# Output rows stored in the order e mod 8, then e div 8, with a DRAM pattern of 16 x 8 rows

## Chip, cores, metric

One core of one Trainium2 chip. The metric is the device time of one execution in microseconds (us); lower is better.

## The reference

For each of the 496 pairs (i, j) of 32 fields, a 1024 x 128 slice of the input is multiplied by a 128 x 128 matrix, and the product is multiplied element by element with the other slice.

```python
# inputs (1024, 32, 128) f32, W (496, 128, 128) f32; I_IDX, J_IDX: the pairs i < j
v_i = inputs[:, I_IDX, :]
v_j = inputs[:, J_IDX, :]
transformed = jnp.einsum('bpd,ped->bpe', v_i, W)
return transformed * v_j            # (1024, 496, 128) f32
```

The output alone has 260 MB.

## The kernel before

An output tile holds e (128 rows of the output of a pair) on the partitions, and for two pairs (`OG = 2`) all 1024 batch elements: 8 KB per partition, 1 MiB per tile. Four such tiles rotate. SyncE issues the stores, the weight loads and nearly all loads of x. The host reorders the result to the reference's layout; this is not timed.

```python
opool = ctx.enter_context(tc.tile_pool(name="o", bufs=4))
...
def load_w(c, splits=(0, WL)):                     # 256 KB: WL = 4 matrices
    ...
        nc.sync.dma_start(out=w_raw[c][:, a:b, :], in_=wt[c, :, a:b, :])
...
def second(u):
    ...
    if k == 0 and h == 0:
        ots[g] = opool.tile([P, OG, BT], F32, tag="ot", name=f"ot_{g}")
    nc.vector.tensor_tensor(ots[g][:, k, s], po.pop(u), x_sb[j][:, s], ALU.mult)
    if q >= NQ - 2:                                # the last two pairs in smaller pieces
        nc.sync.dma_start(out=out[g, :, k, s], in_=ots[g][:, k, s])
    elif k == OG - 1 and h == 1:
        nc.sync.dma_start(out=out[g], in_=ots[g])
...
args.append(nc.dram_tensor("out_0_dram", (NQ // OG, P, OG, BT), F32, kind="ExternalOutput").ap())
...
y[:, perm, :] = got.transpose(3, 0, 2, 1).reshape(BT, NQ, P)
```

## Time and profile before

| | before |
|---|---|
| median | 766.67 us (765.97 to 773.16, 4 runs) |
| DMA engines busy | over 90% in all slices but the last |
| moved | 310 MB, 402 GB/s |
| store of 1 MiB, issue to landing | 8.9 us (median) |
| rows of 8 KB (packet records) | mean 320 ns, median 309; 92% at or under 330, 191 of 31616 at 600 to 609 |
| packets of 2 KB and more in flight (packet records, 20 to 750 us) | 16 in 75% of the time, 15 to 17 in 96% |

The prediction shows the lines that say what bounds the kernel. Three more are needed for the comparison later. The first is from the page's groups (busy us, mean ns; then the idle time just before these instructions and what ended most of it), the second from the page's DMA issues (KB each, us to landing), the third from the view of the output tile (duration of SyncE's issue of a store, ns min/median/max):

```profile
L172 DVE TENSOR_TENSOR ot<-po,x 128x512 f32<-128x512 f32 x992 | 618.6, 684 | 129.5 <-DMA out_dram<-ot 70.2
...
out_dram<-ot SPq DMA_DIRECT2D x247, 1024.0 KB, 8.9
```

```profile
L176 SPq DMA_DIRECT2D out_dram<-ot x247: 332/332/1258, 14.3 to 759.0; - x124
```

### The profile page before, as it was taken

To read this page: it belongs to the slowest core of one execution; us is meant where nothing else is said; L and a number is where in the kernel's file an instruction comes from. 1 tells how busy PE (TensorE), PEld (TensorE's weight loads), DVE (VectorE), ACT (ScalarE), POOL (GpSimd) and SP (SyncE) were. 2 spreads that over 40 slices of the span, in tenths; PEclk is the share of its full clock that TensorE was granted. 3 is DMA by queue.
4 is the path that set the end of the run, shared out by engine and by line. 5 is a ranking of instruction groups with operands and counts; after the bars stand their busy time and mean duration, and the time that the engine had idled before them with its cause. 6 is when DMAs were issued, how large, how long until landed. Compare 5 with 4: busy or idle time off the path is not lost.

```text
span 769.8 us, 11824 instructions
## 1 busy us (share of the span) xinstructions
PE 722.7 (94%) x2946; PEld 545.4 (71%) x2946; DVE 632.0 (82%) x1012; ACT 638.7 (83%) x1256; POOL 593.2 (77%) x863
## 2 busy tenths in 40 slices
PE   7988999999999999999999989999999999999994
PEld 3556766677777676777777767777777777777773
DVE  4869888888888788888888878888888888888885
ACT  2276988888888898888888889998988898998983
POOL 2677998887889878878878696978786969697660
PEclk9999999999999999999999999999999999999998
DMA  9999999999999999999999999999999999999997
GB/s 352 424 419 384 407 397 410 405 400 406 410 405 403 400 409 416 409 379 421 411 414 407 412 403 406 411 407 408 415 410 395 408 410 409 409 408 405 400 401 307
DMA packets 59108, 310.11 MB, mean 403 GB/s; under 512 B 6560, under 2 KB 6816, under 8 KB 27424
## 3 DMA queue, kind: packets, MB, share of 16 engines
q1 hardware_dynamic: 58464, 308.31, 99.4%
q10 hardware_dynamic: 576, 1.05, 0.4%
q8 instruction: 24, 0.39, 0.2%
q14 instruction: 44, 0.36, 0.1%
HBM read 49.28 MB, written 260.05 MB: 402 GB/s over the span
## 4 chain that ended last, share of the span: by engine, by line
DMA 61%; DVE 21%; PE 15%; issue 2%; DVEq 0%; SPq 0%; ACT 0%
DMA out_dram<-ot 60%; DVE ot L172 19%; PE po L157 9%; PE po L166 4%; DVE xd L195 2%; PE po L154 1%; DMA x<-in_xt_dram 1%; DVEq L172 0%; SPq L85 0%; DVEq L217 0%; ACT po L158 0%; DVEq L195 0%
## 5 line engine op out<-in xcount | busy, mean ns | idle before, releaser
L172 DVE TENSOR_TENSOR ot<-po,x 128x512 f32<-128x512 f32 x992 | 618.6, 684 | 129.5 <-DMA out_dram<-ot 70.2
L158 ACT ACTIVATE po<-po 128x512 f32<-128x512 f32 x962 | 551.2, 583 | 106.5 <-PE po L157 53.3
L157 PE MATMUL po<-xh,wh 128*128 128x512 f32 x962 | 388.7, 404 | 24.4 <-DVE ot L172 21.6
L166 PE MATMUL po<-xd,wd 128*128 128x512 f32 x962 | 376.9, 392 | 5.7 <-DVE xd L195 5.7
L157 PE MATMUL po<-xl,wl 128*128 128x512 f32 x962 | 377.6, 392 | 2.2 <-POOL wl L95 2.1
L157 PEld LDWEIGHTS po<-xh,wh 128*128 128x128 f32 x962 | 180.9, 188 | 110.2 <-DVE ot L172 72.5
L95 POOL TENSOR_TENSOR wl<-w,wh 128x256 fp32r<-128x256 f32 x241 | 179.2, 744 | 92.1 <-ACT wh L94 90.7
L166 PEld LDWEIGHTS po<-xd,wd 128*128 128x128 f32 x962 | 181.0, 188 | 46.3 <-ACT po L158 3.8
L157 PEld LDWEIGHTS po<-xl,wl 128*128 128x128 f32 x962 | 181.1, 188 | 36.8 <-POOL wl L95 4.5
L97 POOL TENSOR_TENSOR wd<-wl,wd 128x256 fp32r<-128x256 f32 x241 | 180.0, 747 | 20.1
L96 POOL TENSOR_SCALAR wd<-wh 128x256 fp32r<-128x256 f32 x241 | 99.1, 411 | 20.3
L94 ACT ACTIVATE wh<-w 128x256 fp32r<-128x256 f32 x241 | 99.2, 412 | 0.5 <-DMA w<-in_wt_dram 0.5
L110 POOL TENSOR_TENSOR xl<-x,xh 128x512 fp32r<-128x512 f32 x52 | 67.3, 1293 | 19.8 <-ACT xh L109 19.5
L115 POOL TENSOR_TENSOR xd<-xh,xl 128x512 fp32r<-128x512 f32 x32 | 41.4, 1292 | 2.7
L109 ACT ACTIVATE xh<-x 128x512 fp32r<-128x512 f32 x52 | 32.5, 628 | 10.5 <-DMA x<-in_xt_dram 10.3
L111 POOL TENSOR_SCALAR xl<-xl 128x512 fp32r<-128x512 f32 x52 | 32.8, 631 | 4.6
L154 PE MATMUL po<-x,w 128*128 128x512 f32 x60 | 29.0, 645 | 4.1 <-DMA x<-in_xt_dram 4.1
L154 PEld LDWEIGHTS po<-x,w 128*128 128x128 f32 x60 | 12.1, 206 | 20.2 <-issue 13.9
L195 DVE TENSOR_TENSOR xd<-xh,xl 128x512 fp32r<-128x512 f32 x20 | 16.6, 831 | 0.0
L109 ACT ACT_TABLE_LOAD x1 | 1.3, 1283 | 2.6 <-issue 2.6
L211 POOL MEMSET const-float32-0.0<- 128x1 f32 x1 | 0.1, 98 | 0.2 <-issue 0.2
L211 POOL MEMSET const-bfloat16-1.0<- 128x1 bf16 x1 | 0.1, 101 | 0.0
(2 smaller groups left out, 0.2 us busy)
## 6 DMA issues: line engine op xcount, KB each, us to landing
out_dram<-ot SPq DMA_DIRECT2D x247, 1024.0 KB, 8.9
w<-in_wt_dram SPq DMA_DIRECT2D x123, 256.0 KB, 9.1
x<-in_xt_dram SPq DMA_DIRECT2D x30, 512.0 KB, 9.5
x<-in_xt_dram ACTq DMA_DIRECT2D x4, 256.0 KB, 5.1
out_dram<-ot SPq DMA_DIRECT2D x4, 256.0 KB, 7.0
w<-in_wt_dram SPq DMA_DIRECT2D x1, 192.0 KB, 3.6
w<-in_wt_dram SPq DMA_DIRECT2D x1, 64.0 KB, 2.9
```

What stands on the lines that cost most here:

```text
L94: nc.scalar.mul(h, raw, 1.0 - 2.0**-13)
L95: nc.gpsimd.tensor_tensor(l, raw, h.bitcast(F32), ALU.subtract)
L96: nc.gpsimd.tensor_scalar(d, h.bitcast(F32), EPS, 1.0, ALU.mult, ALU.mult)
L97: nc.gpsimd.tensor_tensor(d, l.bitcast(F32), d.bitcast(F32), ALU.subtract)
L109: nc.scalar.mul(h, x_sb[f][:, s], 1.0 - 2.0**-13)
L110: nc.gpsimd.tensor_tensor(l, x_sb[f][:, s], h.bitcast(F32), ALU.subtract)
L115: nc.gpsimd.tensor_tensor(d, h.bitcast(F32), l.bitcast(F32), ALU.subtract)
L154: nc.tensor.matmul(po[u], w_raw[q // WL][:, q % WL, :], x_sb[i][:, s], start=True, stop=True)
L157: nc.tensor.matmul(po[u], w_s[c][t][:, r], x_s[i][t][:, s], start=t == 0, stop=t == 1)
L158: nc.scalar.mul(po[u], po[u], 1.0 + EPS)
L166: nc.tensor.matmul(po[u], w_s[q // WC][2][:, r], x_s[i][2][:, s], start=False, stop=True, skip_group_check=True)
L172: nc.vector.tensor_tensor(ots[g][:, k, s], po.pop(u), x_sb[j][:, s], ALU.mult)
```

## The change

Its intent is that adjacent rows of DRAM are written at any one time; no record shows which rows are. Row e of a tile goes to place (e mod 8) x 16 + e div 8.

```diff
-            nc.sync.dma_start(out=out[g, :, k, s], in_=ots[g][:, k, s])
+            nc.sync.dma_start(out=out[g, :, :, k, s].rearrange("b a c -> a b c"), in_=ots[g][:, k, s])
         elif k == OG - 1 and h == 1:
-            nc.sync.dma_start(out=out[g], in_=ots[g])
+            nc.sync.dma_start(out=out[g].rearrange("b a k c -> a b k c"), in_=ots[g])
...
-    args.append(nc.dram_tensor("out_0_dram", (NQ // OG, P, OG, BT), F32, kind="ExternalOutput").ap())
+    args.append(nc.dram_tensor("out_0_dram", (NQ // OG, 8, P // 8, OG, BT), F32, kind="ExternalOutput").ap())
...
-    y[:, perm, :] = got.transpose(3, 0, 2, 1).reshape(BT, NQ, P)
+    y[:, perm, :] = got.transpose(4, 0, 3, 2, 1).reshape(BT, NQ, P)
```

Two things change at once: where a row lands, and the shape of the store's DRAM side, from 128 rows to 16 x 8 rows. The shape is called the split below.

## The prediction

It rests on an assumption that the trace of before does not show: with a DRAM side of 16 x 8 rows, the 16 DMA engines fall into eight pairs whose rows hinder each other, so that a row takes twice 309 ns while a pair is in step. Its d is a second assumption: how far a pair is out of step, from 0 (a row takes 309 x 2 ns) to 1 (309 ns), by the form 309 x (2 - d). Three more are assumed: that all engines start a store together, which keeps d small (but in the trace of before the 16 landings of a store lie 4.7 us apart in the median); that with four buffers a pair which runs ahead loses its lead at the next store; and that a store therefore takes as long as its slowest pair. The long rows of which it speaks can be counted: of 1147 rows over 400 ns, 957 belong, in the order of starts, to the stores ahead of a weight load.

> **What bounds the kernel now.** I read the page from the top: the busy shares, the row of DMA shares, the queues, the chain that ended last, then the stretches and the waits. From the page of the kernel before:
>
> ```profile
> span 769.8 us, 11824 instructions
> PE 722.7 (94%) x2946; PEld 545.4 (71%) x2946; DVE 632.0 (82%) x1012; ACT 638.7 (83%) x1256; POOL 593.2 (77%) x863
> ...
> DMA  9999999999999999999999999999999999999997
> ...
> q1 hardware_dynamic: 58464, 308.31, 99.4%
> ...
> HBM read 49.28 MB, written 260.05 MB: 402 GB/s over the span
> ## 4 chain that ended last, share of the span: by engine, by line
> DMA 61%; DVE 21%; PE 15%; issue 2%; DVEq 0%; SPq 0%; ACT 0%
> DMA out_dram<-ot 60%; DVE ot L172 19%; PE po L157 9%; PE po L166 4%; DVE xd L195 2%; PE po L154 1%; DMA x<-in_xt_dram 1%; DVEq L172 0%; SPq L85 0%; DVEq L217 0%; ACT po L158 0%; DVEq L195 0%
> ```
>
> The reader is to see that the 16 DMA engines have no free slice, that one queue fills 99.4% of them, that five sixths of the bytes are stores, and that the store is 60% of the chain. TensorE at 94% looks as tight, but the chain gives it only 15%. Three lines of the table of stretches say that this holds all through (stretch, busy of PE, PEld, DVE, ACT, POOL, then clock, DMA share, GB/s):
>
> ```profile
> 100.00:200.00 100.00, 93.82 (x390) 71.49 (x389) 85.44 (x139) 85.39 (x172) 84.60 (x121) 1.00 1.01 404
> 300.00:400.00 100.00, 96.38 (x398) 72.78 (x397) 81.90 (x133) 87.83 (x173) 80.76 (x119) 1.00 1.01 407
> 600.00:700.00 100.00, 98.31 (x416) 76.85 (x416) 86.05 (x139) 90.09 (x177) 81.08 (x123) 1.00 1.01 408
> ```
>
> The chain in order of time shows the loop of the four output buffers (start us, us, what): a store of 1 MiB takes 8.9 us to land, four products of VectorE refill the buffer, and the next store starts.
>
> ```profile
> 601.03 8.94 DMA out_dram<-ot
> 610.10 2.50 DVE ot L172 x4
> 612.61 8.92 DMA out_dram<-ot
> 621.65 2.50 DVE ot L172 x4
> 624.16 8.93 DMA out_dram<-ot
> ```
>
> One round is 11.58 us and moves four stores and two weight loads, 4.72 MB, so 407 GB/s, as the stretches say. The 8.9 us are mostly queueing behind other stores. The page does not hold the packet records, so I counted them in the trace. A packet is one row. Each of the 247 large stores has 128 rows of 8 KB, so each of the 16 DMA engines moves 247 x 8 = 1976 of them:
> - 8 KB rows: median 309 ns[...]; mean 320; 92% at or under 330. Sum over 16 engines: 632.9 us.
> - 2 KB rows: mean 86 ns, 90.2 us. 4 KB rows: mean 173 ns, 41.4 us. Semaphore writes and instruction fetches: some 5 us.
>
> The sum, 770, is the span. So the time is the sum of the row times on each DMA engine, and anything that changes the time of an 8 KB row goes straight into it.
>
> [...]The trace of before shows 16 packets in flight nearly always[...]8192 B in 309 ns is 26.5 GB/s, and 92% of the rows run at it, so there are no lasting collisions.[...]
>
> **The change part by part.**
> *Removed and added instructions:* none. The order of the changed program against the old one has the same rows on TensorE, VectorE, ScalarE and GpSimd, and the same 405 on SyncE; only the stores differ, with a DRAM side of 16x8x2048 in place of 128x2048. Rows stay 8 KB long, so packets stay 31,616. The transposes in the host code are not timed.
>
> *Issuing:* SyncE may take longer over a pattern with one more dimension. It has room; this line of its waits (us in total, times, longest) is idle time:
>
> ```profile
> SPq L176 <- DVE ot L172: 481.8, 244, 4.4
> ```
>
> Even 0.5 us more for each of 251 stores is 126 us of 482. Cost 0.
>
> *Which engine moves which row:* here lies my choice. The outer DRAM dimension, e div 8, now has 16 values for 16 engines[...]
>
> *Cost in step:* a row takes twice 309, say 606 ns (a value at which rows of the kernel before already pile up when something halves them). 1976 x 606 = 1197 us; with 90 + 41 + 5 for the rest 1333 us.
>
> *Does it stay in step?* [...]So the slowest of eight pairs decides. I set d = 0.15, an estimate: 309 x 1.85 = 572 ns, 1976 x 572 = 1130 us, with 136 for the rest 1266. The timed runs lie 3.7 us under the profiled span (766.1 against 769.8): about 1262.
>
> *HBM side:* sixteen adjacent rows of 8 KB at once instead of rows far apart. The most that better placement could save is the excess over the floor: (320 - 309) x 1976 = 22 us, and I saw that the long rows sit in the last one or two of a store ahead of a weight load, which row order does not touch. I count 0.
>
> **The rivals.**
> - *[...]nothing happens.* [...]For it: rows, packets and bytes are the same, and 92% of the rows are at the floor, so HBM order can do nothing. [...]Time 760 to 772.
> - *The intent works: adjacent rows ease HBM.* All the excess saved is 22 us of 766, 2.9%; TensorE, 98% busy late on, would catch some. Time 745 to 760. Against it: where the long rows stand.
> - *Pairs drift out of step.* With d near a half a row takes 1.5 x 309 = 464 ns: 916 + 136 = 1052. In full opposition the loss is nil. [...]Against it: the slowest pair decides.
> - *HBM is worse too:* all engines in one stretch of 128 KB at the same offset in their rows. Then above 1340. Nothing in the profile speaks for it.
>
> **Range and chances.** The mechanism with d between 0 and 0.5 gives 1050 to 1333; I give it 0.72. Weaker conflicts, 800 to 1050: 0.12. No conflict: 0.13, a sliver of it faster. Worse than 2x: 0.03. Range 970 to 1345. Faster by over 2%: 0.02; within 2%: 0.12; slower: 0.86.
>
> **What would show it.** Right: packets and bytes as before, DMA share still 9 in every slice, but some 240 GB/s; 8 KB rows with a median near 570 to 606 ns; 2 KB and 4 KB rows unchanged; landing of a store about 18 us instead of 8.9; VectorE's wait for the store some 500 us instead of 70; TensorE's instructions as before with idle time between them. Wrong on the split: 8 KB rows still at 309. Wrong on d: rows split between 309 and 606 in equal numbers. Wrong on HBM: rows above 606, or loads slower too.

## The result, and the profile after

848.56 us median (845.13 to 851.18, 4 runs). The ratio to the kernel before is 1.1053, 95% interval 1.0995 to 1.1111. Ratios here are the mean time of one kernel's fast runs over that of the other's of the same rounds, so not quite the ratio of the medians. The change is slower by a tenth: the direction was predicted, the size was not.

From the page of the changed kernel, the lines that answer those of before:

```profile
span 845.2 us, 11824 instructions
PE 747.6 (88%) x2946; PEld 542.0 (64%) x2946; DVE 633.3 (75%) x1012; ACT 649.4 (77%) x1256; POOL 594.6 (70%) x863
...
DMA  9999999999999999999999999999999999999998
...
q1 hardware_dynamic: 58464, 308.31, 100.0%
...
HBM read 49.28 MB, written 260.05 MB: 366 GB/s over the span
...
DMA out_dram<-ot 70%; DVE ot L172 16%; PE po L157 6%; PE po L166 3%; DMA w<-in_wt_dram 1%; DMA x<-in_xt_dram 1%; DVE xd L195 1%; DVEq L172 0%; POOL xd L115 0%; POOL xl L110 0%; ACTq L76 0%; POOL wd L97 0%; POOL wl L95 0%; POOL xl L111 0%; DVEq L217 0%
...
L172 DVE TENSOR_TENSOR ot<-po,x 128x512 f32<-128x512 f32 x992 | 619.5, 684 | 203.8 <-DMA out_dram<-ot 134.3
...
out_dram<-ot SPq DMA_DIRECT2D x247, 1024.0 KB, 10.3
```

Packets (58464) and bytes are the same, the DMA engines are as full as before, yet they move 366 GB/s instead of 402. VectorE's products take the same 684 ns each and wait 134.3 us for stores instead of 70.2. So the same transfers keep the DMA engines busy for longer. The table of stretches shows it in every stage (same columns as in the prediction):

```profile
100.00:200.00 100.00, 88.94 (x363) 66.55 (x362) 79.90 (x129) 80.78 (x161) 75.44 (x108) 0.99 1.01 362
300.00:400.00 100.00, 90.74 (x364) 66.14 (x365) 76.15 (x123) 81.42 (x159) 75.35 (x109) 1.00 1.01 370
600.00:700.00 100.00, 93.11 (x372) 67.25 (x371) 76.74 (x125) 83.71 (x162) 72.70 (x107) 1.00 1.01 366
```

And the loop of the four buffers in the chain of the changed kernel, in order of time; a round takes 13.1 us here (594.19 to 607.32) instead of 11.6:

```profile
594.19 10.49 DMA out_dram<-ot
...
604.80 2.50 DVE ot L172 x4
...
607.32 10.95 DMA out_dram<-ot
```

The packet records of the two traces say which transfers got longer (one packet is one row; sums are over all packets, divided by 16 engines):

| rows | before: mean ns, sum us | after: mean ns, sum us |
|---|---|---|
| 8 KB (stores) | 320, 632.9 | 362, 716.1 |
| 2 KB (nearly all weight loads) | 86, 90.2 | 86, 90.1 |
| 4 KB (loads of x) | 173, 41.4 | 162, 38.9 |

All of the loss is in the stores' rows. Their median is still 309 ns; 8% were over 330 ns before, 18% are now, and 10% of all now lie between 500 and 850 ns.

The records do not name the DMA engine, but the trace holds 16 semaphore increments for each store. I take them as one from each of the 16 engines, when its share has landed. These are the 16 landings of the first three large stores, in us after the first landing of each (from the semaphore records):

```
before  store 1  0 .01 .05 .07 .23 .27 .36 .36 .41 .42 .43 .45 .48 .49 .65 1.26
        store 2  0 .01 .03 .06 .18 .24 .33 .34 .40 .41 .42 .44 .45 .46 .62 1.30
        store 3  0 .02 .03 .07 .18 .23 .32 .35 .38 .40 .40 .42 .45 .47 .61 1.41
after   store 1  0 .04 .10 .10 .11 .20 .26 .29 .32 .32 .34 .37 .40 .41 .44 .53
        store 2  0 .04 .06 .07 .08 .17 .26 .29 | 1.66 1.67 1.72 1.74 1.82 2.04 2.18 2.19
        store 3  0 .04 .08 .13 .15 .25 .27 .30 | 1.79 1.86 2.04 2.05 2.07 2.21 2.22 2.30
```

From the second store on, the landings of the changed kernel mostly come in two groups of eight. Over all 247 stores the gap between the eighth and the ninth landing has a median of 1.23 us (1 us or more in two thirds of the stores); before it is 0.05 us. Eight pairs in which one engine lags its partner would give this. A lag of just four rows (4 x 309 ns = 1.24 us) is not shown: the gap is the distance between the groups, and if the landings are matched in order (first with ninth, second with tenth and so on), the median lag is 1.84 us, six rows.

### The profile page after: what moved, and what is told of

It is laid out like the page before. It is cut to its first block, busy times and chain, and to the rows that moved or that the text cites. A ratio compares the mean times of both kernels' runs of the same rounds, so it can differ in the third digit from the quotient of the medians.

```text
span 845.2 us, 11824 instructions
## 1 busy us (share of the span) xinstructions
PE 747.6 (88%) x2946; PEld 542.0 (64%) x2946; DVE 633.3 (75%) x1012; ACT 649.4 (77%) x1256; POOL 594.6 (70%) x863
## 3 DMA queue, kind: packets, MB, share of 16 engines
q1 hardware_dynamic: 58464, 308.31, 100.0%
## 4 chain that ended last, share of the span: by engine, by line
DMA 72%; DVE 16%; PE 9%; issue 1%; POOL 1%; DVEq 0%; ACTq 0%; ACT 0%; SPq 0%; POOLq 0%
DMA out_dram<-ot 70%; DVE ot L172 16%; PE po L157 6%; PE po L166 3%; DMA w<-in_wt_dram 1%; DMA x<-in_xt_dram 1%; DVE xd L195 1%; DVEq L172 0%; POOL xd L115 0%; POOL xl L110 0%; ACTq L76 0%; POOL wd L97 0%; POOL wl L95 0%; POOL xl L111 0%; DVEq L217 0%
## 5 line engine op out<-in xcount | busy, mean ns | idle before, releaser
L172 DVE TENSOR_TENSOR ot<-po,x 128x512 f32<-128x512 f32 x992 | 619.5, 684 | 203.8 <-DMA out_dram<-ot 134.3
L158 ACT ACTIVATE po<-po 128x512 f32<-128x512 f32 x962 | 553.6, 582 | 170.9 <-PE po L157 107.1
L157 PE MATMUL po<-xh,wh 128*128 128x512 f32 x962 | 399.2, 415 | 72.6 <-DVE ot L172 67.3
## 6 DMA issues: line engine op xcount, KB each, us to landing
out_dram<-ot SPq DMA_DIRECT2D x247, 1024.0 KB, 10.3
w<-in_wt_dram SPq DMA_DIRECT2D x123, 256.0 KB, 10.3
```

What stands on the lines that cost most here:

```text
L157: nc.tensor.matmul(po[u], w_s[c][t][:, r], x_s[i][t][:, s], start=t == 0, stop=t == 1)
L158: nc.scalar.mul(po[u], po[u], 1.0 + EPS)
```

## The experiments

Theory P is that of the prediction: with a DRAM side of 16 x 8 rows the engines hinder each other in pairs over the partitions that they read, whatever the order of the rows in DRAM. Its first rival, H, is that sixteen adjacent rows written at once are slow in HBM. After both had been tested, the question was why the loss is 11% and not the 74% of engines that stay in step (1333 us in the prediction).

### 1. Split and order taken apart

`e1_split_only`: the new split, the old order, with one unused row after each eight. The issue of a store takes 551 ns (median) as in the changed kernel, not 332.

```diff
-            nc.sync.dma_start(out=out[g], in_=ots[g])
+            nc.sync.dma_start(out=out[g, :, 0:8], in_=ots[g])
...                     # the last two pairs and the host's reordering likewise
-  (NQ // OG, P, OG, BT)
+  (NQ // OG, 16, 9, OG, BT)
```

> The stores' DRAM side is 16 x 8 rows as in the changed kernel, but rows keep the old order (e div 8, then e mod 8, each block of 8 rows followed by one unused row[...]). Theory P[...]: 835 to 860 us as the changed kernel, landings of one store in two groups of eight about 1.2 us apart, 8 KB rows with a mean near 360 ns. Theory H (sixteen adjacent rows written at once are slow in HBM): 760 to 775 us, mean near 320 ns, though the landings may be in two groups.

`e2_order_only`: the changed kernel with e mod 4 and e div 4 in place of 8, so a DRAM side of 32 x 4.

```diff
-  (NQ // OG, 8, P // 8, OG, BT)
+  (NQ // OG, 4, P // 4, OG, BT)
```

> Rows in the order e mod 4, then e div 4, with a DRAM side of 32 x 4[...]. Theory P: 760 to 775 us, no two groups of eight among the landings, 8 KB rows near 320 ns. Theory H: 835 us or more, 8 KB rows near 360 ns. A gain by adjacency, the intent of the change: 745 to 760 us.

`e3_pattern_control`: as e1, but 32 x 4 rows (`out[g, :, 0:4]` of a tensor with 32 x 5 rows).

> Control: DRAM side of 32 x 4 rows in the old order, one unused row after each four. If the mere third dimension or the unused rows cost anything, it shows here. P and H both: 760 to 775 us, the 332 ns of the store's issue on SyncE may grow without effect.

`e4_loads_too`: the changed kernel, with the loads of x and w given a DRAM side of 16 x 8 as well. If the loss needs loads and stores of different splits, 770 to 800 us; if stores alone make it, 840 to 860 us.

```diff
-  in_=wt[c, :, a:b, :]
+  in_=wt[c, :, :, a:b, :].rearrange("b a q e -> a b q e")      # likewise for xt; the host lays both out to suit
```

> The changed kernel with the loads of x and w split in the same way as its stores (their DRAM rows stored e mod 8 first, DRAM side 16 x 8). [...]about 770 to 800 us. If it comes from the pairs of stores alone: 840 to 860 us, or more, as the loads now collide among themselves too (2 KB rows above 84 ns for one in five or so).

| run | us, median | ratio to before (95%) | 8 KB rows, mean ns | gap of landings 8 to 9, median us |
|---|---|---|---|---|
| the change | 848.56 | 1.1053 (1.0995 to 1.1111) | 362 | 1.23 |
| e1_split_only | 845.23 | 1.1026 (1.1003 to 1.1048) | 360 | 1.16 |
| e2_order_only | 768.61 | 1.0037 (1.0003 to 1.0071) | 317 | 0.03 |
| e3_pattern_control | 766.83 | 1.0007 (0.9982 to 1.0033) | 317 | 0.04 |
| e4_loads_too | 848.62 | 1.1075 (1.1030 to 1.1120) | 357 | 0.46 |

All four gave correct results. Span, and the row of the DMA issues for the stores, of e1 and then of e2:

```profile
span 844.3 us, 11824 instructions
...
out_dram<-ot SPq DMA_DIRECT2D x247, 1024.0 KB, 10.3
```

```profile
span 763.7 us, 11824 instructions
...
out_dram<-ot SPq DMA_DIRECT2D x247, 1024.0 KB, 8.9
```

The split alone makes the whole loss (1.1026), the order alone none of it (1.0037): H falls. The intent of the change gains nothing in e2 either. The issue of a store takes longer with the three-dimensional pattern (median 332 ns before, 545 ns in e2), without effect on the time. In e4 the loads' rows get longer too (4 KB rows with a mean of 199 ns instead of 162), the stores' rows are a little shorter (a mean of 357 ns), and the total stays: giving loads and stores the same split does not bring the time back.

### 2. Is it the partitions?

`m3_ports` moves data only: 60 stores of 64 partitions back to back, with the first partition at 0, 16, 32 and 0 again. The author took it that under P all rows hinder each other from partition 0 on, half of them from 16 and none from 32. Its output is wrong, which doesn't matter for the time.

```python
for base in (0, 16, 32, 0):
    for n in range(60):
        nc.sync.dma_start(out=out[g, 0:4].rearrange("b a k c -> a b k c"), in_=ots[n % 4][base : base + 64])
        g += 1
    gate()       # VectorE touches all four tiles: the next phase starts when all have landed
```

> Data movement alone, wrong result on purpose: four phases of 60 stores of 64 partitions (512 KB, 16 x 4 rows of 8 KB[...]), back to back; the partitions are 0-63, 16-79, 32-95, and 0-63 again. [...]rows near 606 ns and 2.4 us per store for 0-63, near 600 for half of the rows with 16-79, 309 ns and 1.25 us per store for 32-95. If something else of the new split is to blame (one more dimension, neighbouring rows): the same time in all four phases.

| partitions | us per 512 KB store | 8 KB rows: under 350 ns / over 550 ns |
|---|---|---|
| 0-63 | 2.57 | 5% / 94%, median 629 ns |
| 16-79 | 2.53 | 52% / 48% |
| 32-95 | 1.26 | 98% / 2%, median 309 ns |
| 0-63 again | 2.52 | 3% / 95%, median 628 ns |

The table of stretches of this run (columns: length, busy of DVE and POOL, clock, DMA share, GB/s), one stretch in each phase:

```profile
40.00:160.00 120.00, 0.34 (x2) 0.00 (x0) 1.00 0.99 206
200.00:300.00 100.00, 0.00 (x0) 0.00 (x0) 1.00 0.76 219
340.00:400.00 60.00, 0.69 (x4) 0.00 (x0) 1.00 1.01 384
430.00:520.00 90.00, 0.00 (x0) 0.00 (x0) 1.00 0.97 206
```

The same pattern and bytes run at 206 or at some 400 GB/s depending on the first partition alone. From partition 0 on a row takes some 629 ns, from 32 on 309, and from 16 on half of the rows (48%) are long. (In the stretch from 340 us on the end of the phase drags the mean; 512 KB in 1.26 us are 416 GB/s.) With 16-79 the DMA share is 0.76, so there some engines are idle part of the time; the trace does not say which. So collisions that follow the partitions as expected are shown; at what place on the chip the rows meet, and which engine takes which partition, is not, as no record names either.

### 3. In step, and out of step

`m_before` and `m_after`: data movement alone, with the stores in the old and in the changed form. The code is condensed. `gate()` is as above; because it goes through the tiles in order, three of four stores in the phases with a gate after each start alone, and the fourth starts behind its predecessor.

```python
for n in range(40): gate(); store(g, ots[n % 4]); g += 1          # 1: one at a time
gate()
for n in range(80): store(g, ots[n % 4]); g += 1                  # 2: back to back
gate()
for n in range(80):                                               # 3: a 256 KB load after every second
    store(g, ots[n % 4]); g += 1
    if n % 2 == 1: load_w(n // 2)
gate()
for n in range(20): store(g, ots[n % 4]); g += 1; load_w(40 + n); gate()     # 4
```

P1 is that stores hinder each other and that pairs which get out of step get free; P2 that stores do not hinder each other, but a load that is under way does.

> No arithmetic, wrong result on purpose: stores of 1 MiB in the old form in four phases. (1) 40 stores one at a time, each waited for; (2) 80 stores back to back; (3) 80 stores with a 256 KB weight load after every second; (4) 20 times one store and one load together, waited for. All theories: 8 KB rows at 309 ns in phases 1 and 2, 2.45 to 2.5 us per store in phase 2; the turn to a load in phases 3 and 4 stretches the last one or two rows.

> The same with the stores in the changed form. Theory P1[...]: phase 1 rows near 606 ns, as every store starts with all engines in step, and a store lands some 2.4 us later than in the old form; phase 2 starts slow and gets to 2.5 us per store when the pairs have drifted apart, landings in two groups of eight. Theory P2[...]: phases 1 and 2 as in the old form, 309 ns, and only phases 3 and 4 slower, with 8 KB rows of 500 to 800 ns while loads run.

| phase | us per store, old form | changed form | 8 KB rows, mean ns, old / changed |
|---|---|---|---|
| 1 one at a time | 3.89 | 5.88 | 318 / 473 |
| 2 back to back | 2.50 | 2.51 | 315 / 315 |
| 3 with loads | 2.86 | 3.27 | 313 / 365 |
| 4 store and load together | 4.42 | 6.40 | 372 / 522 |

From the chain in order of time, stores that start alone, m_before and then m_after (start us, us from issue to landing):

```profile
47.29 3.87 DMA out_dram<-ot
...
51.53 3.86 DMA out_dram<-ot
```

```profile
109.95 6.19 DMA out_dram<-ot
...
116.51 6.19 DMA out_dram<-ot
```

A stretch of phase 1, 2 and 3 each, m_before and then m_after:

```profile
40.00:170.00 130.00, 13.29 (x134) 0.00 (x0) 1.00 0.67 276
200.00:360.00 160.00, 0.00 (x0) 0.00 (x0) 1.00 1.01 419
400.00:590.00 190.00, 0.17 (x1) 0.00 (x0) 1.00 1.02 421
```

```profile
40.00:240.00 200.00, 13.33 (x136) 0.00 (x0) 1.00 0.65 178
280.00:440.00 160.00, 0.00 (x0) 0.00 (x0) 1.00 1.01 420
500.00:690.00 190.00, 0.00 (x0) 0.00 (x0) 1.00 1.01 367
```

A store that starts alone takes 2.3 us longer (6.19 against 3.86). By the packet records of the stores at 109.95 us (m_after) and 51.53 us (m_before), 0.4 us of this is a later first row (1.20 us after the issue instead of 0.83), and 2.0 us are longer rows, where a full doubling would be 2.47 us (8 x 309 ns). Most of the first rows take 596 to 640 ns. But the doubling does not last through even one store: in the order of their starts, the first 64 of its 128 rows have a mean of 629 ns, the last 64 of 401, and many of these are at 309 again. So the collision is partly over after 64 of the 128 rows, four per engine if each moves eight.

Back to back the changed form loses nothing: 420 GB/s against 419, rows with a mean of 315 ns in both. The landings of a store then spread over 2.8 us without a gap in the middle (eighth to ninth 0.26 us); matched in order, the lag is 1.28 us, about four rows. Pairs that no longer hinder each other at such a lag would give this. Two things keep it from being shown. The records name no engine. And in `m4_after` (section 5) the third to the sixth store, back to back, have all 16 landings within 0.8 to 0.9 us, so no pair can lag by four rows at the landing, and yet the rows between 17.5 and 27.5 us have a mean of 312 ns; there the lag grows to 1.22 us only in the course of 40 stores. How small a lag already avoids the collision, and why, stays open. So does the very first store of the changed kernel: its first 96 of 128 rows, in the order of their starts, took 309 to 318 ns, and its landings came within 0.53 us, where stores that start alone in the data-movement run took some 600 ns for their first rows. It was issued at 13.6 us and its first rows came at 19.7 us, behind loads; whether that is why was not tested.

With a load after every second store the loss is back at 0.41 us per store (3.27 - 2.86), and the rate of 367 GB/s is that of the full changed kernel. P1 holds, as far as it says that stores hinder each other and get free of it, though not in two groups of landings; P2 (loads alone collide with stores) falls with phase 1.

Around one load in phase 3 of m_after the packet records show how it goes. I counted the rows under way every 0.2 us. Between loads 16 rows are at 309 ns (563.0 to 564.4 us). In the 1.4 us before the first engines come to their load, eight rows are long and eight are not. While eight engines load (from 566.2 us), the eight other rows are long, and for some 1.2 us after it eight are long and eight are not. Then the other engines load, some seven rows are long once more for 0.6 us, and 16 are fast again. Whether each engine has its long rows once per load, the roles exchanged, can't be told without the engines' names.

### 4. What of a load costs?

`m2_before` and `m2_after`: six phases of 40 stores each.

```python
for every, many in ((1, 1), (2, 1), (4, 1), (4, 2)):       # phases 1 to 4: loads after so many stores, so many loads
    ...
# 5: as phase 2, with the load split as the changed stores: wt[c].rearrange("(b a) q e -> a b q e", a=16)
# 6: no load, but gate() after every second store
```

> Data movement alone, old form of the stores, wrong result on purpose; six phases of 40 stores: a 256 KB load after every store; after every second; after every fourth; two loads after every fourth; after every second, the loads split over the engines as the changed stores are; no loads, but a wait for all after every second store. All theories: the stores take 2.50 us each and each load some 0.7 us.

> The same with the stores in the changed form. Theory T (each turn from stores to a load and back puts the pairs into collision for a few rows): the extra over the old form goes with the number of turns, some 0.8 us per turn: 32 us, 16, 8, 8 (two loads at one turn cost what one does), 16. Theory W (the load's own writes collide with the other engines' store reads): the extra goes with the bytes loaded: 32, 16, 8, 16, and the fifth phase differs from the second[...]. Theory S (being put in step by a common start is what costs): only the sixth phase and the first stores of each phase have it, about 2 us per common start, 40 us in the sixth.

| phase | turns | old form, us | changed form, us | extra | per turn |
|---|---|---|---|---|---|
| 1: a load after every store | 40 | 125.8 | 153.5 | 27.7 | 0.69 |
| 2: after every second | 20 | 112.7 | 127.8 | 15.1 | 0.76 |
| 3: after every fourth | 10 | 110.4 | 117.6 | 7.2 | 0.72 |
| 4: two after every fourth | 10 | 117.4 | 121.9 | 4.5 | 0.45 |
| 5: as 2, loads in the new split | 20 | 117.5 | 125.9 | 8.4 | 0.42 |
| 6: a common start after every second | 20 | 117.7 | 154.5 | 36.8 | 1.84 |

These are read from the records to a microsecond or so. The extra goes with the number of interruptions (phases 1 to 3), not with the bytes loaded: phase 4 loads as much as phase 2 and loses less than half. W falls in this, and S, which had only some 2 us in each of the phases 1 to 5, falls too. T is not right in full: it expected 8 us in phase 4 (4.5 came) and 16 in phase 5, where loads in the new split lose 8.4 instead of 15.1. So the split of a load matters as well, which W alone had expected. Much of that difference is in the base: the same loads cost the old form 4.8 us more (117.5 against 112.7). Phase 6 repeats what a common start costs.

The full kernel says the same. `e5_before_wide_w` and `e6_after_wide_w` load the weights 512 KB at a time, 62 loads instead of 124, in the kernel before and in the changed one.

```diff
-WL = 4
+WL = 8
-WLEAD = 4
+WLEAD = 2
-rpool ... bufs=5, wpool ... bufs=4
+rpool ... bufs=3, wpool ... bufs=3
...                     # and two loads at the start go
```

> The kernel before with weights loaded 512 KB at a time instead of 256 KB (62 loads instead of 124; fewer weight buffers to make room). 755 to 785 us; a base for the next run, and faster than the kernel before by up to 10 us if turns from store to load cost it something.

> The changed kernel with weights loaded 512 KB at a time. Theory T: the loss against the run with the same loads and old stores falls from 80 us to 45 to 55 us, since 62 of the 154 turns are gone. Theory W: the loss stays at 75 to 85 us, as the bytes loaded are the same.

Both are correct: 772.09 us (768.5 to 773.76) and 821.74 us (817.0 to 828.27), so the loss is 49.7 us, inside the 45 to 55 that theory T expected, against 81.9 us (848.56 - 766.67) with small weight loads. Per load (62 + 30 of x, and 124 + 30) these are 0.54 and 0.53 us. The two groups of landings are not needed for the loss: in e6 the gap from the eighth to the ninth has a median of 0.16 us. The hoped-for gain of larger loads in the old form did not come: e5 is 1.0059 times before (1.0020 to 1.0099); its fewer weight buffers may be why, which was not tested.

### 5. Is it the change of direction?

`m4_before` and `m4_after`: 40 stores per phase, and after every second one something of another kind (the code is condensed).

```python
if kind == "old":   nc.sync.dma_start(out=OLD, in_=t)     # store of 256 KB, 128 rows
elif kind == "new": nc.sync.dma_start(out=NEW, in_=t)     # store of 256 KB, 16 x 8 rows
elif kind == "small": nc.sync.dma_start(out=wts[c][:, 0:1, :], in_=wt[c, :, 0:1, :])     # load of 64 KB
elif kind == "big": nc.sync.dma_start(out=big[c % 6], in_=xt[:, c : c + OG, :])          # load of 1 MiB
```

> Base, data movement alone, wrong result on purpose: five phases of 40 stores of 1 MiB in the old form, with after every second: nothing; a store of 256 KB split as the old stores; one split as the changed stores; a load of 64 KB; a load of 1 MiB. About 101 us for nothing, and 20 times 0.64, 0.64, 0.2 to 0.4 and 2.5 us more in the others.

> The same with the 1 MiB stores in the changed form. Theory D (the change of direction at a turn undoes the lag of four rows): extra over the base near 0 for the small stores, 12 to 16 us for 20 loads of 64 KB and for 20 of 1 MiB alike. Theory L (any transfer that is not a whole store shifts the pair): 10 to 20 us for the small stores in the old split, and less for loads of 64 KB, which shift it by 0.2 us only. The small stores in the changed split [...]0 to 10 us.

| after every second store | old form, us | changed form, us | extra, us (each of 20) |
|---|---|---|---|
| nothing | 98.1 | 100.1 | 2.0 |
| store of 256 KB, old split | 114.3 | 138.9 | 24.6 (1.23) |
| store of 256 KB, new split | 127.4 | 129.0 | 1.6 (0.08) |
| load of 64 KB | 102.4 | 107.1 | 4.7 (0.24) |
| load of 1 MiB | 152.1 | 178.4 | 26.3 (1.32) |

The phase limits are sure to some 2 us, so extras of 1.6 and 2.0 us can't be told from nothing. Theory D (the change from a store to a load) falls: a small store in the old split has no change of direction and costs more (1.23) than a load of the same 256 KB does (0.76 in phase 2 of m2). The small store in the new split costs nothing that can be seen on top of the new-split stores around it; it does cost 13.1 us among old-split stores (127.4 against 114.3), where its own 2 KB rows have a mean of 129 ns instead of 87. So among stores it is the other split that costs. L fits this better, and the small cost of a 64 KB load. It does not give the sizes: the old-split stores cost 24.6 us where it expected 10 to 20, and two loads of 256 KB in a row cost less (0.45) than one (0.72) and than one of 1 MiB (1.32). Nor does it carry over to loads: given the stores' split, they still cost 0.42 us each (m2, phase 5) and the kernel its full loss (e4). Why a load brings the collisions back, and how its length sets the loss, stays open.

## Why the prediction was wrong

- **What bounds the kernel: right.** The sum of row times is again the span (851 us of rows, 845 us of span), and everything lost is in the 8 KB rows.
- **No other instructions, same packets, issue without effect: right.** (SyncE issues 406 DMAs in both traces, not 405.) The issue grew from 332 to 551 ns (median), and the order-only run had that too (545 ns) at no cost (1.0037).
- **That the split makes rows hinder each other, and that it depends on the partitions: right in all that was tested.** Split only gives the loss (1.1026), order only does not (1.0037), and in `m3_ports` rows take 629 or 309 ns by the first partition. Why this split does it was not shown.
- **The HBM side counted 0: right.** Order only is at 1.0037.
- **Cost in step, 606 ns per row: right.** 596 to 640 ns for most first rows of a store that starts alone, 629 ns (median) with partitions 0-63 in `m3_ports`.
- **"Does it stay in step?": this step failed.** I took one lag d for the whole run, argued that "the slowest of eight pairs decides", and set d = 0.15. The runs show that a pair does not stay in step: when a store starts alone, its rows are long for about half of it (a mean of 629 ns, then 401), and back to back the loss vanishes (2.51 against 2.50 us per store). Only something else between the stores brings a loss, some 0.5 us for each of 154 loads in this kernel. What frees the pairs was not shown, only that they get free.
- The term in the sum was therefore mis-sized: 572 ns for a row, measured 362. With 362 the sum comes out at 851 us (1976 x 362 = 715, and 136 for the rest), against a span of 845.2. Taking off another 3.7 us, as the prediction did, compared two executions: the profiled one of before was timed at 771.7 us, 1.9 above its own span of 769.8, and the other three of that time at 766 to 767.
- The form 309 x (2 - d) failed as well, and not only d = 0.15. In `m4_after` the third to the sixth store have landings at most 0.91 us apart, so d is at most 0.74 (0.91 of 1.236 us, four rows of 309 ns), if the lag at the landing is the lag that counts and four rows are a full lag, both assumptions of mine. The form then gives 390 ns or more, and the rows measured 312.
- The rival "pairs drift out of step" was nearest to the truth; I had named it and let the slowest pair overrule it. The trace of before shows no pairs (a gap of 0.05 us from the eighth to the ninth landing). But it could have warned of one premise, that all engines start a store together: its 16 landings of a store lie 4.7 us apart in the median, nearly two stores.
- Of the signs that the prediction listed, packets, DMA share and unchanged rows of the loads came; 240 GB/s (366), a landing of 18 us (10.3) and a wait of 500 us (134.3) did not, all for the same reason. The median of the 8 KB rows stayed at 309 ns, which the prediction had listed as the sign of a wrong split; as the experiments show (1.1026 for the split alone), it was not.

No run beat the kernel before. The best of the variants, the pattern control, is at 1.0007.

## What to carry to other kernels

The shape of the DRAM side of a store can cost time by itself: with 128 partitions on chip, an outer DRAM count of 32 or 128 kept this kernel at full rate (768.61 and 766.83 us, and 766.67), and an outer count of 16 cost a tenth, in either order of the rows (848.56 and 845.23 us). `m3_ports` points to the partitions that are read: stores of 64 partitions in one pattern took 2.57 us from partition 0 on (rows of 629 ns) and 1.26 us from 32 on (309 ns). When transfers hinder each other, do not assume that they stay in step or that the worst pair decides; measure the in-step cost and the settled cost by themselves, since here they are a factor of two (629 ns against 309 at the start of a store) and nothing (2.51 against 2.50 us per store back to back). And where most rows already take their shortest time (92% of rows here at or under 330 ns, with a median of 309), look for what another row order could gain before you write it: here it gained nothing (1.0037).
